# A graph attention layer on one core: the first turn waits for the one-hot, and SyncE fetches the rows of one tile in every 14th pair

## The chip, the cores and the metric

One core of one Trainium2 chip runs the kernel. The metric is the device time of one execution in microseconds (us); lower is better. The engines are TensorE (PE; its weight loads are listed apart as PEld), VectorE (DVE), ScalarE (ACT), GpSimd (POOL) and SyncE (SP). A DMA is issued by an engine's queue (SPq, ACTq, POOLq) and carried by the core's 16 DMA engines.

## The reference

12500 nodes with 128 features, 400000 edges sorted by their destination, 32 features an edge, 8 heads of 16 channels. Cut to what matters:

```python
x_l = (ln1(h) @ W_l).reshape(n, 8, 16)          # h = relu(layernorm(x))
x_r = (ln1(h) @ W_r).reshape(n, 8, 16)
e = (ea @ W_e).reshape(-1, 8, 16)               # each edge; each node has a loop with the mean of ea as well
m = leaky_relu(x_l[src] + x_r[dst] + e, 0.2)
alpha = einsum('ehc,hc->eh', m, att)
a = softmax of alpha over the edges of each dst
out = segment_sum(x_l[src] * a[:, :, None], dst, n) + bias
h = h + out
ff = gelu(ln2(h) @ W1 + b1) @ W2 + b2
return x + h + ff
```

## The kernel before

**Prologue.** For about 190 us the node statistics are made, the lists of sources and destinations come in, and x_l is written to a table in DRAM, `xl_dram`, one row of 512 bytes for each node.

**Edges.** The edges are cut into tiles of 128 and pairs of 512 (four tiles, j = 0 to 3); there are 782 pairs. Four pairs share one set of loads ("windows"), eight pairs make one batch of the softmax. A round is the time step of the schedule, one for each pair: `window_edges` writes the order of all engines out by hand, round by round, and each step has its own lag against the pair it works on. A tile framework turns the reads and writes into semaphore waits. Each engine carries out its own instructions strictly in order. What happens to pair c:

- *windows* (SP, round c-4, for four pairs at once): `words` reads the offset of the four pairs into a register (L1000, a TENSOR_LOAD), then come the DMAs of edge features `ea` (L1069), local destinations `dl` (L1074) and x_r's rows `zw` (L1079), each into one of a few buffers that TensorE has to have freed.
- *gather* (POOL, four rounds ahead or more): one indirect DMA for each tile (L1033) takes 128 rows of `xl_dram` into the slot of the pair in `ring`, which has 30 slots. A slot is free when the sums of the pair 30 before are done. 29 pairs, the "raw" ones, get their rows by one plain DMA of SP in place of the four gathers.
- *place* (DVE, round c-1): the one-hot of the destinations is written beside the edge features in `ea` (L1100).
- *combine* (PE, round c): four "turns" transpose the four tiles of gathered rows into a bank of PSUM (L1127), and one product of `zw` with `ea` closes z = x_l[src] + x_r[dst] + ea W_e in the same bank (L1132). The profile counts each z product as two instructions and each sum of a tile as two.
- *slope* (ACT, L1150), *bend* (DVE, L1164) and *score* (PE, L1185) are the leaky relu and the product with att.
- For each batch of eight pairs: scans over the sorted edges (DVE, L1193 to L1214), the exponential (ACT, L1218), the turn of the weights back (PE `t`, L1225) and a copy of them (ACT, L1235).
- *times* (DVE, L1246, round c+12): the rows in the ring are multiplied by their weights, in place, 512 columns in one operation.
- *collect* (PE, L1277, round c+13): the weighted rows are summed over destinations, into `sums`; ACT copies these to `rec` (L1289), and a DMA on ACT's queue (L1308), 24 rows at an address from a register, brings them to `state`.

Beside this run the steps of the groups of nodes (x_r for later nodes, and the feed-forward part for nodes that are done), with loads and stores of their own on SP's queue.

A "tell" is a semaphore increment by which an instruction says that it is done. The framework gives one to each instruction that another engine's instruction waits for.

Of the kernel before, what the change touches and what calls it, by code (L numbers as in the profile page):

```python
# [13 lines left out]
F32 = mybir.dt.float32  # L14
# [53 lines left out]
BUSY = 5  # L68
LEAD = 2
KEPT = 7  # L70
BIG = 2.0**100
CAP = 2.0**120

# [59 lines left out]
def raw_pairs(nt, n_edges):  # L133

    n_pr = -(-n_edges // (UP * U))
    at = [xr_round(t, nt, n_edges) + XR_STEPS + 1 + RAW_LATER for t in range(GN, nt, GN)]
    at = at[:-1] + [r + RAW_SHIFT for r in at[:RAW_MORE]]
    return [(r + RAW_STEPS + AHEAD + 1, r) for r in at if r + RAW_STEPS + AHEAD + 2 < n_pr]


def heads_of(nc, pool, out, att_c, fh):
# [8 lines left out]
def tile_gnn(  # L150
# [56 lines left out]
    idx_sb = keep.tile([P, IDX, NB * K], I32, name="idx_sb")  # L207
    NQU = NU // QU
    at_sb = keep.tile([1, NQU + BEHIND, 1 + QP], I32, name="at_sb")
    dst_sb = keep.tile([P, NCH * K], I32, name="dst_sb")  # L210
    local_sb = dst_sb.bitcast(F32)
    flag = keep.tile([1, 1], I32, name="flag")
# [69 lines left out]
    def from_pairs(a, b):  # L282

        ps = once_ps.tile([P, GN * P], F32, name="w_ps")
        nc.tensor.matmul(ps[:, 0 : b - a], pick, firsts[:, a:b], start=True, stop=True)
        nc.vector.tensor_tensor(
            local_sb[:, a * K : b * K].rearrange("p (c j) -> p c j", j=K),
            dst_sb[:, a * K : b * K].rearrange("p (c j) -> p c j", j=K),
            ps[:, 0 : b - a, None].to_broadcast([P, b - a, K]),
            op=OP.subtract,  # L290
        )

    first_sb = build.tile([1, NU // UP], I32, name="first_sb")
# [497 lines left out]
    with tc.manual_schedule():  # L791
        load_first()
        make_identity(nc, ident)
        load_weights()
        load_x(0, min(GN, NT))
        load_raw()
        load_x(GN, min(3 * GN, NT - GN))
        for t in range(4 * GN, NT, 14):
            load_x(t, min(14, NT - t))
        load_dst()  # L800
        load_consts()
        nc.vector.memset(empty, 0.0)
        rows_at = [i * 5 // 4 for i in range(len(raw))]
        for r in range(max(max(len(qs), 9) + LAST + 1, 16 + PARTS, rows_at[-1] + KEPT + 1)):
            if r == 0:
                count_up()
            for d, at in zip(raw, rows_at):
                if r == at:
                    raw_gather(d)
                if r == at + KEPT:  # L810
                    raw_store(d)
            if r == 3:
                weights()
            if r == 9:
                last_of_units()
            if r == 14:
                nc.sync.dma_start(src_sb, src)
                nc.sync.dma_start(
                    idx_sb[:, 0 : IDX - 1], src[:, 0 : (IDX - 1) * NB * K].rearrange("p (b k) -> p b k", b=IDX - 1)
                )  # L820
            if r == 10:
# [33 lines left out]
    with tc.If(fast == 1) as cmp:  # L855
        window_edges(
            tc, n_edges, ea_t, NT, NE, NUE, ident, wer, weh, zneg, nodes, local_sb, bias_r, b2_r, w1_sb, w2_sb,
            cols, xl_dram, xl_t, xr_dram, xr_t, dc_dram, g_dram, late_dram, state_dram, state, clear, xr_steps, qs, raw_steps, raw, x_t, out_t, bend_x, src, idx_sb, at_sb, wid,
        )
    with cmp.Else():  # L860
        with tc.tile_pool(name="any_h", bufs=1) as any_h:
# [69 lines left out]

def window_edges(
    tc, n_edges, ea_t, NT, NE, NUE, ident, wer, weh, zneg, nodes, local_sb, bias_r, b2_r, w1_sb, w2_sb,
    cols, xl_dram, xl_t, xr_dram, xr_t, dc_dram, g_dram, late_dram, state_dram, state, clear, xr_steps, qs, raw_steps, raw, x_t, out_t, bend_x, src, idx_sb, at_sb, wid,
):


# [41 lines left out]
    with ExitStack() as es:  # L979
# [25 lines left out]
        def rows_at(t, at, n, size):  # L1005

            return t.rearrange("n f -> (n f)").bitcast(U8)[ds(at, n * size)].rearrange("(n f) -> n f", f=size)

        def slot(c):
# [15 lines left out]
        def gather(c):  # L1025
            if c in of_raw:
                rows = nc.sync.dma_start(slot(c)[:, :, 0:P], late_dram[of_raw[c]["i"]])
                pairs[c]["rows"] = [rows.ins]
                return
            pairs[c]["rows"] = []  # L1030
            for t in tiles_of(c):
                for j in t:
                    rows = nc.gpsimd.indirect_dma_start(  # L1033
                        out=slot(c)[:, j, 0:P],
                        out_offset=None,
                        in_=xl_dram,
                        in_offset=bass.IndirectOffsetOnAxis(ap=index(c, j), axis=0),
                    )
                    behind_last(rows, c - RING)
                    pairs[c]["rows"].append(rows.ins)  # L1040
# [56 lines left out]
        def place(c):  # L1097

            d = pairs[c]
            placed = nc.vector.tensor_scalar(  # L1100
                d["ea"][0:WN].rearrange("p (a b) -> p a b", b=OW),
                d["dl"][0:WN].rearrange("p (a b) -> p a b", b=OS)[:, :, 0:OW],
                wid[0:WN], None, op0=OP.is_equal,
            )
# [17 lines left out]
        def combine(c):  # L1122
# [6 lines left out]
                ).ins  # L1129
                for j in range(e // P)  # L1130
            ]
            d["closed"] = nc.tensor.matmul(z[:, :e], d["zw"], d["ea"][:, :e], start=False, stop=True).ins  # L1132
            d["z"] = z
            for ins in d["loads"]:
# [105 lines left out]
        def times(c):  # L1240

            b, i = batch_at[c]
            weights = of_batch[b]["t"].rearrange("p (j w i h) -> p j w i h", j=KP, w=2, i=NB)[:, :, 0, i : i + 1]
            k = sum(len(t) for t in tiles_of(c))
            rows = slot(c)[:, 0:k, 0:P].rearrange("p j (c h) -> p j c h", h=H)
            product = nc.vector.tensor_tensor(  # L1246
                rows, rows, weights[:, 0:k].to_broadcast([P, k, C, H]), op=OP.mult
            )
            pairs[c]["products"] = [product.ins]
            for ins in (*pairs[c]["turns"], *pairs[c]["rows"]):  # L1250
                tc.declare_no_dep(
                    product.ins, ins, reason="TensorE waited for it ahead of the turned weights, which are read here"
                )

        def own_nodes(q):
            d = of_four[q]
# [932 lines left out]
```

## Time and profile before

| | |
|---|---|
| timed runs | 4845.96, 4851.8, 4852.41 us; median 4851.8 |
| the profiled execution | 4798.29 us, its span 4796.5 us |
| granted TensorE clock, mean | 0.875 |
| PE, DVE, POOL, ACT busy | 3544.8, 2622.4, 2952.7, 1502.6 us |
| DMA | 425616 packets, 536.78 MB, 112 GB/s |

How to read the lines below: a group of instructions is given as line, engine, operation, output <- input and count, then busy time and mean ns of one, then the idle time of the engine just before them and what ended most of it. In the chain that ended last each piece is followed back to what released it; "issue" is time in which an engine waited for nothing that the profile shows, "remote" or "another core or an unknown queue" a wait whose releaser the profile cannot name. A row of one line has the durations as min/median/max in ns. A row of windows has start and end, length, busy time with the number of instructions for each engine, granted clock, share of the DMA engines and GB/s. A row of the waits has total us, times and the longest.

### The profile page before, as it was taken

What the parts mean: (1) busy time and instruction counts of PE and PEld (TensorE: products, weight loads), DVE (VectorE), ACT (ScalarE), POOL (GpSimd) and SP (SyncE); (2) the same over time, 40 slices, a digit from 0 to 9 for tenths busy, and PEclk for the clock granted to TensorE, in tenths of its full rate; (3) what the DMA queues carried; (4) which work ended last, traced back from release to release, by engine and by line L of the source; (5) the groups of instructions that cost most, each with busy time, mean ns of one, the idle gap of its engine ahead of it and who ended that gap; (6) DMA issues with size and microseconds to landing.
All of it is one profiled execution on the core that took longest, in us unless ns stands there. A gap on an engine that the chain in (4) does not pass through costs nothing.

```text
span 4796.5 us, 48948 instructions
## 1 busy us (share of the span) xinstructions
PE 3544.8 (74%) x14951; PEld 1790.8 (37%) x14952; DVE 2622.4 (55%) x4977; ACT 1502.6 (31%) x3825; POOL 2952.7 (62%) x3136
## 2 busy tenths in 40 slices
PE   3327777777777777777777877777778777777787
PEld 2203333333333333343333433333434333333344
DVE  5316555655655555556555555555555555555455
ACT  5302323322322323323333333333333333333222
POOL 6655666665666666666666666666666666666650
PEclk8658888888888989899898989898989898889898
DMA  6525555555543443444434334343344433434331
GB/s 185 164 75 151 141 145 144 148 146 147 142 132 93 112 110 102 104 112 105 106 93 106 100 98 102 98 101 101 91 99 108 100 100 98 102 86 103 100 96 31
DMA packets 425616, 536.78 MB, mean 112 GB/s; under 512 B 97241, under 2 KB 307210, under 8 KB 424794
## 3 DMA queue, kind: packets, MB, share of 16 engines
q1 hardware_dynamic: 282360, 266.19, 21.5%
q0 software_dynamic: 100000, 205.00, 16.5%
q10 hardware_dynamic: 42984, 62.37, 4.4%
q8 instruction: 121, 1.98, 0.2%
q14 instruction: 151, 1.24, 0.1%
HBM read 471.82 MB, written 61.42 MB: 111 GB/s over the span
## 4 chain that ended last, share of the span: by engine, by line
PE 38%; DVE 20%; another core or an unknown queue 15%; issue 12%; ACT 5%; DMA 2%; POOL 1%; ACTq 1%; SPq 0%; DVEq 0%; POOLq 0%
PE sums L1277 12%; PE z L1132 9%; PE s L1185 7%; PE z L1127 6%; DVE ea L1100 3%; DVE ring L1246 3%; DVE m L1164 3%; DVE s L1193 2%; DVE p L1207 2%; POOL ring L1033 1%; DVE p L1200 1%; ACT zs L1150 1%; ACT rec L1289 1%; PE acc L1612 1%
## 5 line engine op out<-in xcount | busy, mean ns | idle before, releaser
L1033 POOL DMA_INDIRECT ring<-xl_dram,idx_sb x3009 | 2839.8, 944 | 1637.4 <-issue 785.4
L1277 PE MATMUL sums<-ring,own 128*32 128x144 f32 x6250 | 1044.9, 317 | 979.2 <-ACT rec L1289 645.2
L1277 PEld LDWEIGHTS sums<-ring,own 128*32 128x32 f32 x6250 | 681.8, 119 | 1551.7 <-ACT rec L1289 801.2
L1164 DVE TENSOR_TENSOR m<-z,zs 128x512 f32<-128x512 f32 x782 | 532.8, 681 | 900.7 <-issue 538.8
L1132 PE MATMUL z<-ea,zw 128*128 128x512 f32 x1564 | 920.2, 674 | 10.9 <-issue 7.4
L1185 PE MATMUL s<-m,zneg 128*64 128x512 f32 x1564 | 851.2, 636 | 90.9 <-issue 71.4
L1150 ACT ACTIVATE zs<-z 128x512 f32<-128x512 f32 x782 | 464.8, 594 | 1171.5 <-PE z L1132 303.7
L1246 DVE TENSOR_TENSOR ring<-ring,t 128x512 f32<-128x512 f32 x782 | 527.8, 676 | 391.8 <-PE t L1225 179.4
L1127 PE MATMUL z<-ident,ring 128*128 128x128 f32 x3125 | 594.1, 320 | 25.2 <-DMA raw_dram<-raw 11.5
L1100 DVE TENSOR_SCALAR ea<-dl,wid 96x516 f32<-96x516 bf16 x782 | 577.7, 739 | 15.1 <-DMA zw<-xr_dram 15.1
L1289 ACT COPY rec<-sums 32x144 f32<-32x144 f32 x782 | 204.8, 262 | 1103.7 <-remote 332.0
L1127 PEld LDWEIGHTS z<-ident,ring 128*128 128x128 f32 x3125 | 379.8, 158 | 243.0 <-issue 218.1
L1185 PEld LDWEIGHTS s<-m,zneg 128*64 128x64 f32 x1564 | 165.7, 142 | 758.2 <-issue 635.0
L1193 DVE TENSOR_TENSOR_SCAN s<-g,s 64x512 f32<-64x512 bf16 x98 | 120.4, 1228 | 332.0 <-remote 100.6
L1132 PEld LDWEIGHTS z<-ea,zw 128*128 128x128 f32 x1564 | 279.3, 223 | 11.9 <-issue 8.0
L1259 DVE TENSOR_TENSOR own<-nodes,sums 128x512 f32<-128x512 f32 x195 | 132.6, 680 | 246.3 <-remote 190.0
L1218 ACT ACTIVATE p<-p 64x512 f32<-64x512 f32 x98 | 61.7, 630 | 330.0 <-DVE p L1207 128.8
L1235 ACT COPY ring<-t 128x256 f32<-128x256 f32 (+3 forms) x236 | 65.7, 344 | 253.7 <-DVE ring L1246 150.6
L326 POOL DMA_INDIRECT raw<-in_x,lead x92 | 88.9, 967 | 52.0 <-issue 26.6
L1207 DVE TENSOR_TENSOR_SCAN p<-g,s 64x512 f32<-64x512 bf16 x98 | 119.8, 1222 | 1.5
L1336 DVE TENSOR_REDUCE part<-ea_s 128x1 f32<-128x1024 f32 x98 | 118.3, 1207 | 0.0
L1218 ACT ACT_TABLE_LOAD x66 | 84.7, 1283 | 1.2
(244 smaller groups left out, 2248.5 us busy)
## 6 DMA issues: line engine op xcount, KB each, us to landing
dl<-dc_dram SPq DMA_DIRECT2D x196, 396.0 KB
ea_s<-in_ea_t ACTq DMA_DIRECT2D x98, 512.0 KB
ea<-in_ea_t SPq DMA_DIRECT2D x196, 256.0 KB
ring<-xl_dram,idx_sb POOLq DMA_INDIRECT x3009
state<-empty SPq DMA_DIRECT2D x98, 144.0 KB
f_st<-state SPq DMA_DIRECT2D x48, 288.0 KB
state<-rec ACTq DMA_DIRECT2D x782, 13.5 KB
zw<-xr_dram SPq DMA_DIRECT2D x196, 48.0 KB
```

What stands on the lines that cost most here:

```text
L1033: rows = nc.gpsimd.indirect_dma_start(out=slot(c)[:, j, 0:P], out_offset=None, in_=xl_dram, in_offset=bass.IndirectOffsetOnAxis(ap=index(c ...
L1100: placed = nc.vector.tensor_scalar(d["ea"][0:WN].rearrange("p (a b) -> p a b", b=OW), d["dl"][0:WN].rearrange("p (a b) -> p a b", b=OS)[:, ...
L1127: nc.tensor.matmul(z[:, j * P : (j + 1) * P], row_of(c, j)[:, 0:P], ident, start=(j == 0), stop=False, is_transpose=True).ins
L1132: d["closed"] = nc.tensor.matmul(z[:, :e], d["zw"], d["ea"][:, :e], start=False, stop=True).ins
L1150: sloped = nc.scalar.activation(d["zs"][:, :e], d["z"][:, :e], AF.Copy, scale=SLOPE)
L1164: bent = nc.vector.tensor_tensor(d["m"][:, :e], d["z"][:, :e], d["zs"][:, :e], op=OP.max)
L1185: d["score"] = nc.tensor.matmul(of_batch[b]["s"][0:HB, :e], zneg[:, k : k + HB], d["m"][:, :e], start=(i == 0), stop=(c == batches[b][-1]) ...
L1193: nc.vector.tensor_tensor_scan(d["s"][HB:P], d["g"][:, 0:EPR], d["s"][0:HB], BIG, op0=OP.add, op1=OP.min)
L1207: nc.vector.tensor_tensor_scan(d["p"][0:HB, back], d["g"][:, 1 : EPR + 1][:, back], d["s"][HB:P][:, back], BIG, op0=OP.add, op1=OP.min)
L1246: product = nc.vector.tensor_tensor(rows, rows, weights[:, 0:k].to_broadcast([P, k, C, H]), op=OP.mult)
L1277: nc.tensor.matmul(sum_at[c % PLACES], own[:, c % QP * KP + j, :], slot(c)[:, j, :], start=(j == js[0]), stop=(j == js[-1]),).ins
L1289: nc.scalar.copy(d["rec"], sum_at[c % PLACES])
```

## The change

**The first turn waits.** `place` keeps its instruction, and `combine` gives the first turn of each pair a dependency on it. The product that closes z then has nothing left to wait for. With that most turns lose their tells: in the two built programs the turns tell 2286 times before and 159 times after, and TensorE in all 5254 and 3148 times.

On PE, around one pair of z bank 1653 to 1655 (before), with the semaphores that each row waits for (DMASW: a gather has landed; DVE, Activation: VectorE, ScalarE):

```order
1790 L1277 MATMUL sums<-ring,own 32x144 x3
1791 L1127 MATMUL z_1655<-ident,ring 128x128 [waits DMASW4_49]
1792 L1127 MATMUL z_1655<-ident,ring 128x128 [waits DMASW5_49]
1793 L1127 MATMUL z_1655<-ident,ring 128x128 [waits DMASW6_49]
1794 L1127 MATMUL z_1655<-ident,ring 128x128 [waits DMASW7_49]
1795 L1132 MATMUL z_1655<-ea,zw_1645 128x512 [waits DVE_49]
1796 L1277 MATMUL sums<-ring,own 32x144 [waits DVE_49,Activation_49]
```

The same place after, where turns are L1210, the closing product L1220 and the sums L1373:

```order
1796 L1373 MATMUL sums<-ring,own 32x144 x3
1797 L1210 MATMUL z_1662<-ident,ring 128x128 [waits DMASW7_49,DVE_49]
1798 L1210 MATMUL z_1662<-ident,ring 128x128 [waits DMASW0_49]
1799 L1210 MATMUL z_1662<-ident,ring 128x128 [waits DMASW1_49]
1800 L1210 MATMUL z_1662<-ident,ring 128x128 [waits DMASW2_49]
1801 L1220 MATMUL z_1662<-ea,zw_1652 128x512
1802 L1373 MATMUL sums<-ring,own 32x144 [waits DVE_49,Activation_49]
```

VectorE's wait has moved from the closing product to the first turn; a second semaphore of one instruction takes an extra step in the queue, and there are 605 of these before the turns after the change (26 before).

**Rows by hand.** For the pairs 30, 44, 58, ... (54 of them) the fourth tile is not gathered by GpSimd. SyncE fetches its 128 rows with 128 DMAs of one row (512 bytes), each at an address from a register, into one of three tiles `hand0` to `hand2`. The addresses come from `hand_sb`, a list of offsets that is built in the prologue (a memset and a copy on DVE, a transpose on PE, a product on DVE), 16 at a time by a TENSOR_LOAD. The rows of a tile are spread over 14 rounds, from 20 to 7 rounds ahead of its pair, half of a round's nine or so at its start and half at its end. One round ahead of the pair SP waits until all 128 have landed. The fourth turn reads the hand tile, and `times` becomes two operations, one of three tiles and one of the hand tile into the ring. In all 6912 row DMAs, 432 loads of 16 words, and 54 gathers less.

On SP, from one windows step to the next (L1000 is `words`, L767 clears state, L685 loads x_r rows), before:

```order
242 L1000 TENSOR_LOAD at_sb
243 L1069 DMA ea<-in_ea_t 32x4x512 [waits DMAHW5_49,PE_49]
244 L1074 DMA dl_1647<-dc_dram 96x2112 [waits DMAHW0_49]
245 L1079 DMA zw_1646<-xr_dram 96x512 [waits DMAHW1_49]
246 L767 DMA state<-empty 128x2x144 [waits DMAHW2_49]
247 L685 DMA xr_4398<-raw_dram 128x512 [waits DMAHW6_49,PE_49,Activation_49]
248 L1000 TENSOR_LOAD at_sb
249 L1069 DMA ea<-in_ea_t 32x4x512 [waits DMAHW1_49,PE_49]
```

and such a stretch after (L1044 is `words`, L1082 a row by hand, L1152 to L1162 the windows, L805 and L723 as L767 and L685):

```order
384 L1152 DMA ea<-in_ea_t 32x4x512 [waits DMAHW7_49,DVE_49,PE_49]
385 L1157 DMA dl_1654<-dc_dram 96x2112 [waits DMAHW0_49]
386 L1162 DMA zw_1653<-xr_dram 96x512 [waits DMAHW1_49]
387 L1082 DMA hand_6198<-xl_dram 1x512 x5
388 L805 DMA state<-empty 128x2x144 [waits DMAHW2_49]
389 L1082 DMA hand_6198<-xl_dram 1x512 x7
390 L1044 TENSOR_LOAD hand_sb
391 L1082 DMA hand_6198<-xl_dram 1x512 x16
392 L1044 TENSOR_LOAD hand_sb
393 L1082 DMA hand_6198<-xl_dram 1x512 x8
394 L723 DMA xr_6513<-raw_dram 128x512 [waits DMAHW1_49,PE_49,Activation_49]
395 L1044 TENSOR_LOAD at_sb
```

36 rows and two loads of offsets now stand between the windows of four pairs and the next.

The diff, cut to its core:

```diff
+HAND_LEAD = 6
+HAND_READ = 16
+HAND_EVERY = 14
+HAND_FIRST = 30
+LANDED = 7
...
+        def hand(r, w, share=(0, 1), behind=0):
+            hands, n = w["pairs"], w["sems"]
+            i, k = divmod(r + HAND_LEAD + hands.step - hands[0], hands.step)
+            if share[0] == 0:
+                w["new"].clear()
+                if k == HAND_LEAD - 1 and 0 < i <= len(hands):
+                    all_here = w["queue"].wait_ge(w["landed"][(i - 1) % n], ((i - 1) // n + 1) * P * 16)
+                    tc.declare_fence(all_here.ins, group=f"{w['name']}{i - 1}")
...
+            first, last = P * k // hands.step, P * (k + 1) // hands.step
+            for e in range(*(first + int((last - first) * x) for x in share)):
+                if e % HAND_READ == 0:
+                    d["at"] = words(
+                        hand_sb[w["at"] + i : w["at"] + i + 1, e : min(e + HAND_READ, P)], (NT * P - 1) * XW * 4,
+                        w["engine"],
+                    )
+                row = w["queue"].dma_start(
+                    d["x"][e : e + 1, :].bitcast(U8), rows_at(xl_dram, d["at"][e % HAND_READ], 1, XW * 4)
+                )
+                row.then_inc(w["landed"][i % n], 16)
...
         def row_of(c, j):
-            return slot(c)[:, j, 0:P]
+            return by_hand[c]["x"] if c in by_hand and j == KP - 1 else slot(c)[:, j, 0:P]
...
                 for j in t:
+                    if c in by_hand and j == KP - 1:
+                        continue
                     rows = nc.gpsimd.indirect_dma_start(
...
-            placed = nc.vector.tensor_scalar(
+            d["placed"] = placed = nc.vector.tensor_scalar(
...
+            tc.add_manual_dep(
+                nc.get_inst_by_name(d["turns"][0].name), d["placed"].ins.name,
+                mybir.DependencyInfo(mybir.DependencyClass.Sync, mybir.DependencyReason.DATA),
+                reason="the product that closes z reads the one-hot and waits for nothing itself",
+            )
             d["closed"] = nc.tensor.matmul(z[:, :e], d["zw"], d["ea"][:, :e], start=False, stop=True).ins
...
+            n = sum(len(t) for t in tiles_of(c))
+            whole = n - 1 if c in by_hand else n
+            for js, x in ((slice(0, whole), None), (slice(whole, n), by_hand.get(c))):
...
+                product = nc.vector.tensor_tensor(
+                    rows,
+                    rows if x is None else x["x"][:, None, :].rearrange("p j (c h) -> p j c h", h=H),
+                    weights[:, js].to_broadcast([P, k, C, H]),
+                    op=OP.mult,
+                )
...
             for r in range(-AHEAD, max(last_round, groups[-1]["round"] + 19)):
+                hand(r, ways[0], (0, 0.5))
                 in_round(r, early, groups[:-2])
...
+                hand(r, ways[0], (0.5, 1))
```

More of the change, by code (lines that the diff above doesn't have):

```diff
@@ L70 @@
 KEPT = 7
+HAND_LEAD = 6
[3 more added lines that the diff above has]
+LANDED = 7
+HAND_ROUND = 24
 BIG = 2.0**100
@@ L138, in raw_pairs, with hand_pairs @@
     return [(r + RAW_STEPS + AHEAD + 1, r) for r in at if r + RAW_STEPS + AHEAD + 2 < n_pr]
+def hand_pairs(nt, n_edges):
+    late = {c for c, _ in raw_pairs(nt, n_edges)}
+    hands = range(HAND_FIRST, n_edges // (UP * U), HAND_EVERY)
+    assert not late & set(hands)
+    return hands
 def heads_of(nc, pool, out, att_c, fh):
@@ L290, in from_pairs, with hand_columns, hand_turn, hand_bytes @@
             op=OP.subtract,
+        )
+    hand_f = build.tile([P, len(hands)], F32, name="hand_f")
+    hand_ps = {}
+    def hand_columns():
+        nc.vector.memset(hand_f, 0.0)
+        for at, h in ((0, hands),):
+            first = (h[0] + 1) * UP * KU - 1
+            step = h.step * UP * KU
+            nc.vector.tensor_copy(
+                hand_f[:, at : at + len(h)], src_sb[:, first : first + step * (len(h) - 1) + 1 : step]
+            )
+    def hand_turn():
+        hand_ps["t"] = once_ps.tile([P, GN * P], F32, name="w_ps")
+        nc.tensor.transpose(hand_ps["t"][0 : len(hands), 0:P], hand_f, ident)
+    def hand_bytes():
+        nc.vector.tensor_scalar(
+            hand_sb, hand_ps["t"][0 : len(hands), 0:P], float(XW * 4), None, op0=OP.mult
         )
@@ L857, in tile_gnn @@
             tc, n_edges, ea_t, NT, NE, NUE, ident, wer, weh, zneg, nodes, local_sb, bias_r, b2_r, w1_sb, w2_sb,
-            cols, xl_dram, xl_t, xr_dram, xr_t, dc_dram, g_dram, late_dram, state_dram, state, clear, xr_steps, qs, raw_steps, raw, x_t, out_t, bend_x, src, idx_sb, at_sb, wid,
+            cols, xl_dram, xl_t, xr_dram, xr_t, dc_dram, g_dram, late_dram, state_dram, state, clear, xr_steps, qs, raw_steps, raw, x_t, out_t, bend_x, src, idx_sb, at_sb, hand_sb, hands, wid,
         )
@@ L933, in window_edges @@
     tc, n_edges, ea_t, NT, NE, NUE, ident, wer, weh, zneg, nodes, local_sb, bias_r, b2_r, w1_sb, w2_sb,
-    cols, xl_dram, xl_t, xr_dram, xr_t, dc_dram, g_dram, late_dram, state_dram, state, clear, xr_steps, qs, raw_steps, raw, x_t, out_t, bend_x, src, idx_sb, at_sb, wid,
+    cols, xl_dram, xl_t, xr_dram, xr_t, dc_dram, g_dram, late_dram, state_dram, state, clear, xr_steps, qs, raw_steps, raw, x_t, out_t, bend_x, src, idx_sb, at_sb, hand_sb, hands, wid,
 ):
@@ L1007, in rows_at @@
             return t.rearrange("n f -> (n f)").bitcast(U8)[ds(at, n * size)].rearrange("(n f) -> n f", f=size)
+        ways = (
+            {"pairs": hands, "at": 0, "queue": nc.sync, "engine": SP, "name": "hand", "sems": LANDED, "new": []},
+        )
+        by_hand = {c: {} for w in ways for c in w["pairs"]}
+        for w in ways:
+            w["landed"] = [tc.alloc_semaphore(f"{w['name']}_landed{i}") for i in range(w["sems"])]
+        def hand(r, w, share=(0, 1), behind=0):
[6 more added lines that the diff above has]
+                    tc.declare_fence(all_here.ins, group=f"{w['name']}{i - 1}")
+            i, k = divmod(i * hands.step + k - behind, hands.step)
+            if not 0 <= i < len(hands):
+                return
+            d = by_hand[hands[i]]
+            if k == 0 and share[0] == 0:
+                d["x"] = once.tile([P, XW], F32, name=f"{w['name']}{i % 3}")
+            first, last = P * k // hands.step, P * (k + 1) // hands.step
[7 more added lines that the diff above has]
+                    d["x"][e : e + 1, :].bitcast(U8), rows_at(xl_dram, d["at"][e % HAND_READ], 1, XW * 4)
+                )
+                row.then_inc(w["landed"][i % n], 16)
+                tc.no_tile_sem_insts.add(row.ins.name)
+                tc.add_to_no_dep_group(f"{w['name']}{i}", row.ins)
+                w["new"].append(row)
         def slot(c):
@@ L1243, in times @@
             weights = of_batch[b]["t"].rearrange("p (j w i h) -> p j w i h", j=KP, w=2, i=NB)[:, :, 0, i : i + 1]
[L1244 to L1252, printed above, removed]
-                )
+            n = sum(len(t) for t in tiles_of(c))
+            whole = n - 1 if c in by_hand else n
+            for js, x in ((slice(0, whole), None), (slice(whole, n), by_hand.get(c))):
+                k = js.stop - js.start
+                if k == 0:
+                    continue
+                rows = slot(c)[:, js, 0:P].rearrange("p j (c h) -> p j c h", h=H)
+                product = nc.vector.tensor_tensor(
[3 more added lines that the diff above has]
+                    op=OP.mult,
+                )
+                pairs[c].setdefault("products", []).append(product.ins)
+                for ins in (*pairs[c]["turns"], *pairs[c]["rows"]):
+                    tc.declare_no_dep(
+                        product.ins, ins, reason="TensorE waited for it ahead of the turned weights, which are read here"
+                    )
         def own_nodes(q):
```

10 lines of the change are left out of this document (added).

## The prediction

> **What bounds the kernel now.** I read the page first: busy time, the chain that ended last, the costly groups.
>
> ```profile
> span 4796.5 us, 48948 instructions
> PE 3544.8 (74%) x14951; PEld 1790.8 (37%) x14952; DVE 2622.4 (55%) x4977; ACT 1502.6 (31%) x3825; POOL 2952.7 (62%) x3136
> ...
> PE 38%; DVE 20%; another core or an unknown queue 15%; issue 12%; ACT 5%; DMA 2%; POOL 1%; ACTq 1%; SPq 0%; DVEq 0%; POOLq 0%
> ...
> L1033 POOL DMA_INDIRECT ring<-xl_dram,idx_sb x3009 | 2839.8, 944 | 1637.4 <-issue 785.4
> L1277 PE MATMUL sums<-ring,own 128*32 128x144 f32 x6250 | 1044.9, 317 | 979.2 <-ACT rec L1289 645.2
> ...
> L1132 PE MATMUL z<-ea,zw 128*128 128x512 f32 x1564 | 920.2, 674 | 10.9 <-issue 7.4
> ...
> L1150 ACT ACTIVATE zs<-z 128x512 f32<-128x512 f32 x782 | 464.8, 594 | 1171.5 <-PE z L1132 303.7
> L1246 DVE TENSOR_TENSOR ring<-ring,t 128x512 f32<-128x512 f32 x782 | 527.8, 676 | 391.8 <-PE t L1225 179.4
> L1127 PE MATMUL z<-ident,ring 128*128 128x128 f32 x3125 | 594.1, 320 | 25.2 <-DMA raw_dram<-raw 11.5
> L1100 DVE TENSOR_SCALAR ea<-dl,wid 96x516 f32<-96x516 bf16 x782 | 577.7, 739 | 15.1 <-DMA zw<-xr_dram 15.1
> ...
> L1127 PEld LDWEIGHTS z<-ident,ring 128*128 128x128 f32 x3125 | 379.8, 158 | 243.0 <-issue 218.1
> ```
>
> No engine is full. The chain is 38% TensorE, 20% VectorE, and 27% time in which the trace names no worker ("another core or an unknown queue", "issue"). TensorE idles 979.2 us ahead of the sums, mostly for ScalarE's rec, and ScalarE idles 1171.5 us ahead of the slope, mostly for TensorE's z. So the pace is a loop of short steps handed between engines, and how soon a handover arrives matters.
>
> One such handover, from the timeline:
>
> ```profile
> 2523.13 1.02 PE L1132 MATMUL z<-ea,zw 128*128 128x512 f32 x2
> ...
> 2526.02 0.27 ACT L1289 COPY rec<-sums 32x144 f32<-32x144 f32 x1 [4.58 <-PE s L1185]
> ...
> 2531.66 0.60 ACT L1150 ACTIVATE zs<-z 128x512 f32<-128x512 f32 x1 [5.38 <-remote]
> ...
> 2533.06 1.23 DVE L1193 TENSOR_TENSOR_SCAN s<-g,s 64x512 f32<-64x512 bf16 x1 [10.88 <-remote]
> ```
>
> The product z is over at 2524.15, the slope that reads it begins at 2531.66 though ScalarE had nothing to do for 5.38 us. The records end early or TensorE's tell arrives late; nothing else is named.
>
> Then the pace, by windows over one stage (first the closing products alone, then the gathers alone):
>
> ```profile
> 1500.00:2500.00 1000.00, 203.89 (x350) 61.26 (x348) 0.90 0.41 106
> 1500.00:2500.00 1000.00, 640.83 (x681) 0.90 0.41 106
> ```
>
> 350 halves of z are 175 pairs in 1000 us: 5.71 us a pair, 80 us for 14 pairs. A gather costs GpSimd 0.944 + 785.4/2554 = 1.25 us, so 681 take 851 us: GpSimd has 15% to spare. What it waits for says the same:
>
> ```profile
>   PE sums L1277: 190.6, 47
> ...
>   PEld z L1127: 13.0, 29
> ```
>
> It stands still because a ring slot is not yet free (first line), while the turns wait only 13.0 us in all for gathered rows (second line). The gathers run ahead; they do not set the end.
>
> **The first turn waits for the one-hot, and turns tell no more.** Who waited for the one-hot:
>
> ```profile
>   PEld z L1132: 3.9, 1
>   PE z L1132: 3.5, 1
> ```
>
> One wait of 3.9 us in 782 products: VectorE places a pair a round ahead, so moving this wait four turns (about 1 us) earlier costs nothing and its removal from z gains at most 4 us; I put 0. Behind the waiting turn stand z, the score and the next sums, so if VectorE fell behind by more than it does now, all of them would wait; the cover is VectorE's 45% of idle time.
>
> What changes is how many times TensorE tells: counted in the two built programs, the semaphore increments fall from 5254 to 3148, those of the turns from 2286 to 159: 2127 fewer. No row prices one tell. From below: nothing, since a group of four turns, each telling, is not issued wider than untold ones (only 25.2 us of idle before 3125 turns). From above: a semaphore step on TensorE's own queue,
>
> ```profile
> L1277 PEldq EVENT_SEMAPHORE  x489: 51/51/51, 368.5 to 4754.9; - x163
> ```
>
> 51 ns, 2127 × 0.051 = 108 us. A tell sits on the same engine, so I price it at this row, and count it where TensorE is on the chain: 38% of 108 = **-41 us**. A loss by fewer tells I exclude: nobody waits for a turn alone but the ring's next gather and VectorE's product, both of which wait for later work anyway. The page "TensorE: Matmul & The Clock Gate", section "The cost: per-tile semaphore tail", of the Trainium skill gives about 26 ns for each increment of a tile's tail and calls a single one on the last matmul sound; by it the term would be 38% of 56, -21 us, and no row here tells the two prices apart.
>
> The price for it: the first turn now waits for two semaphores (gather and one-hot), and the second costs a step of its own in the queue: 605 more, × 51 ns = 31 us. Hidden where the queue runs ahead of the array; the weight load of the turns idles 218.1 us by "issue" in some 750 gaps, so it is not always ahead. Between 0 and 31, again by the chain's 38%: **+12 us**.
>
> **54 tiles fetched by SyncE.** GpSimd drops 54 of 3009 gathers, 54 × 1.25 = 67 us of its time. It waits for ring slots, so this becomes more waiting: **0** (bounds 0 and -67).
>
> VectorE multiplies such a pair in two operations, three tiles and one. A 512-column product takes 676 ns; two of 384 and 128 share the columns, and the second adds a fixed part that no row isolates; between 0 and a quarter of the whole (169 ns). 54 × 0.169 = 9 us at most, by VectorE's 20% of the chain **+2 us**. The four operations that build the list of offsets stand in the prologue, once, beside the node statistics' 128-row work: 0. The bytes: 54 × 64 KB in 6912 packets against 425616 packets now: 0.
>
> SyncE is the open question. It gets 6912 one-row DMAs and 432 loads of 16 words; each tile's are spread over 14 pairs' time. Rows for its prices:
>
> ```profile
> L1000 SPq TENSOR_LOAD <-at_sb x196: 3/412/1009, 194.6 to 4692.9; - x196
> L1000 ACTq TENSOR_LOAD <-at_sb x196: 485/1100/1399, 374.8 to 4760.8; - x196
> ...
> L1308 ACTq DMA_DIRECT2D state<-rec x782: 307/309/1126, 377.7 to 4764.7; - x196
> ...
> L1069 SPq DMA_DIRECT2D ea<-in_ea_t x196: 157/334/656, 195.4 to 4701.8; - x196
> L1074 SPq DMA_DIRECT2D dl<-dc_dram x196: 310/423/962, 195.7 to 4702.2; - x196
> L1079 SPq DMA_DIRECT2D zw<-xr_dram x196: 3/352/1449, 196.8 to 4702.7; - x196
> ...
> SPq L1069 <- PE z L1132: 746.1, 63, 22.3
> ```
>
> A row's DMA: nearest is the state write at a register's address, 24 rows, 309 ns (ends 157 and 423). A load: one word 0.41 us, four words (on ScalarE) 1.10, at best 0.485; so 0.12 to 0.28 us a word, 1.9 to 4.4 us for 16. SyncE's own work: per four pairs 0.41 + 0.33 + 0.42 + 0.35 = 1.5 us, 5.3 per 14, and its other moves about as much again; I put 12 us. In 80 us then: 128 × 0.309 = 40, eight loads 16 to 35, own 12: 68 to 87 us. At the ends of the DMA's price 48 to 101. The nearest row with the smaller load fits, with the larger it doesn't. I take that it fits, since SyncE today waits at the windows until TensorE frees a buffer (last row, up to 22.3 us at a time): its loads come a whole four of pairs early, and a lateness below that is free: **0**. What is queued behind the rows on SyncE: the windows of four pairs (with about 37 rows and two or three loads between them), limits, indices, the clearing of state, the group's loads and stores. The wait for a landed tile comes five rounds (28 us) after its last row was issued: 0.
>
> **Sum.** -41 + 12 + 2 = -27 us: the profiled execution of 4798.29 us (span 4796.5 and 1.8 around it) would become 4771. That execution is 1.1% under the median of the timed runs, 4851.8; the same step from there gives **4825 us**.
>
> **Rivals.**
> 1. *SyncE becomes the bound* (slower). Place: its queue between two windows. It decides once rows, loads and own work pass 80 us per 14 pairs, that is, with rows at 309 ns, loads above 3.5 us. At 4.4 us the excess is 7 us for each of 54 tiles: +378, 5230 us. If only now and then a window comes late, 1 to 2 us for each tile: 4906 to 4960. For it: the median of four words; SyncE works in order, so rows stand still whenever a window waits. Against: waits of up to 22.3 us ahead of the windows now. The page "Runtime: NRT & Kernel Launch" of the Trainium skill, section "Instruction fetch mechanics", gives about 200 ns for each register loaded, even in bulk; by that a load is 3.2 us, the sum 78 of 80 us, which speaks against the change more than the small end of my rows does.
> 2. *The tells cost nothing* (no change): issue does not widen for them, and the 27% without a named worker has another cause. +12 at most, +2 at least: 4854 to 4866; or 4852 with the queue's steps hidden too.
> 3. *GpSimd counts after all* (faster). If ring waits fed back into the gathers' start, 67 us less: 4851.8 - 67 - 27 = 4758 us. Against: 13.0 us of turns waiting for rows.
> 4. *The second semaphore in full*, 31 us, with no gain: 4885 us.
>
> **How the numbers follow.** Forecast 0.44, with a range of its own from 4790 to 4850; rival 1 0.22, half of it above 4960; rival 2 0.18; rival 3 0.10; rival 4 0.06. About 10 us (0.2%) is what a measurement of this kernel can tell from no change. Faster: 0.40 of the forecast and rival 3, 0.50; same: 0.04 and 0.16 of rival 2, 0.20; slower: the rest, 0.30. The range goes down to the tells at their full 108 us (4851.8 - 108 + 2 = 4746) and up to the milder form of rival 1 (4960); some 0.16 lies outside.
>
> **What would show it.** Right: the closing product has no idle time by VectorE, ScalarE's waits for z and rec shrink by some tens of us, the gathers' idle time ahead of ring slots grows by about 67 us, SyncE's longest waits for z at the windows shrink but stay. Wrong: the one-hot or z waits for the DMAs of ea, dl or zw (rival 1), turns wait for SyncE's landed tile, the turns' weight loads idle more by "issue" (rival 4), or the span falls with the gathers (rival 3). The prediction fails most likely on the price of a 16-word load or of a tell, neither of which this trace holds.

## The result, and the profile after

The changed kernel took 5476.7 us (median of 4, 5462.14 to 5484.27) where the kernel before took 4848.88 on the same chip: ratio 1.130, 95% interval 1.127 to 1.133. It is 13% slower. I had forecast 4825 us, a little faster, with a range up to 4960: wrong in sign and by far in size.

One thing has to be known for all that follows. The experiments ran on chips of two kinds. On one kind the kernel before takes 4781 to 4849 us, on the other 3989 to 3990, with the same program. I call them the slower and the faster chip. They are different chips: of those with a number on record, 1, 7 and 11 were of the faster kind, 0, 9 and 15 of the slower. The forecast, its trace and the result above are of the slower kind; the number of that chip is not on record. Each ratio is against the kernel before, measured beside it on the same chip.

The page of the changed kernel, lines that answer to those before:

```profile
span 5475.5 us, 63991 instructions
PE 3693.7 (67%) x14952; PEld 1854.0 (34%) x14953; DVE 2629.5 (48%) x5034; ACT 1488.8 (27%) x3825; POOL 2900.8 (53%) x3082
...
L1116 POOL DMA_INDIRECT ring<-xl_dram,idx_sb x2955 | 2787.3, 943 | 2359.8 <-PE sums L1373 1095.0
...
L1238 ACT ACTIVATE zs<-z 128x512 f32<-128x512 f32 x782 | 464.0, 593 | 1844.2 <-DMA state<-empty 670.2
L1220 PE MATMUL z<-ea,zw 128*128 128x512 f32 x1564 | 962.0, 702 | 2.1 <-issue 2.0
...
L1183 DVE TENSOR_SCALAR ea<-dl,wid 96x516 f32<-96x516 bf16 x782 | 578.4, 740 | 489.1 <-DMA zw<-xr_dram 281.1
...
L1210 PE MATMUL z<-ident,hand 128*128 128x128 f32 x54 | 21.0, 389 | 162.8 <-SPq L1067 92.5
...
PE 2%; SPq 1%; DVE 1%; issue 1%; ACT 0%; DMA 0%; POOL 0%; ACTq 0%; DVEq 0%
```

The last line is the chain that ended last. Here it breaks off after 5% of the span, so it doesn't name what sets the pace; the waits have to. TensorE's busy time grew by 149 us, at a granted clock of 0.835 in place of 0.875, and that of the other engines hardly moved; the rest of the loss is waiting. The gathers wait longer for the ring (1637.4 us of idle became 2359.8), so GpSimd is further from the end than before. The one-hot, which idled 15.1 us, now idles 489.1, mostly for `zw` to arrive: a windows load comes late. The hand tile itself is late too: its turns idle 162.8 us, mostly for SyncE's wait (L1067). The one-hot's wait for `zw` and the turns' wait for the hand tile were the signs I had named for SyncE as the bound. The closing product idles 2.1 us, as planned.

SyncE's queue, waits and instructions of the changed kernel:

```profile
SPq L1152 <- remote: 114.6, 5, 72.9
...
SPq L1152 <- PE z L1220: 12.2, 6, 8.0
...
L1044 SPq TENSOR_LOAD <-hand_sb x432: 3/1247/1561, 358.7 to 5341.2; - x144
...
L1082 SPq MOVE hand<-xl_dram x6912: 1/29/1452, 360.0 to 5350.1; - x198
L1082 SPq DMA_DIRECT2D hand<-xl_dram x6912: 1/228/1466, 360.1 to 5350.2; - x198
```

At the windows SyncE used to wait 746.1 us for z; 12.2 are left. The 114.6 us stand almost wholly before the first row. All waits of SyncE's queue together fall from 2908 to 356 us. It has hardly any slack left, and the rows run from 360 to 5350 us with no gap above 11 us. A row is two instructions, a MOVE of 29 ns and a DMA of 228, by their medians; but the maxima are 1.45 us for either. The medians mislead: in this stretch of the timeline (start, length, line, count)

```profile
2507.75 9.07 SPq L1082 DMA_DIRECT2D hand<-xl_dram  x12
```

twelve rows take 9.07 us, 0.76 us a row. From the start of one row to the start of what follows it, over all 6912 rows, the mean is 0.531 us; for the loads of 16 words it is 1.14. So a tile costs SyncE 128 × 0.531 + 8 × 1.14 = 77 us. Its other work takes 11.8 us more, and on semaphores it waits 3.6, together 92.4 us ((5350 - 360)/54), for 14 pairs that took 80 us before. A queue that waits 3.6 of 92.4 us is full: that is the new pace.

### The profile page after: what moved, and what is told of

It reads as the page before. It is cut to its first block, busy times and chain, and to the rows that moved or that the text cites. A ratio compares the mean times of both kernels' runs of the same rounds, so it can differ in the third digit from the quotient of the medians.

```text
span 5475.5 us, 63991 instructions
## 1 busy us (share of the span) xinstructions
PE 3693.7 (67%) x14952; PEld 1854.0 (34%) x14953; DVE 2629.5 (48%) x5034; ACT 1488.8 (27%) x3825; POOL 2900.8 (53%) x3082
## 5 line engine op out<-in xcount | busy, mean ns | idle before, releaser
L1116 POOL DMA_INDIRECT ring<-xl_dram,idx_sb x2955 | 2787.3, 943 | 2359.8 <-PE sums L1373 1095.0
L1373 PE MATMUL sums<-ring,own 128*32 128x144 f32 x6250 | 1078.9, 324 | 1215.9 <-ACT rec L1385 718.4
L1373 PEld LDWEIGHTS sums<-ring,own 128*32 128x32 f32 x6250 | 699.0, 122 | 1833.6 <-ACT rec L1385 967.9
L1220 PE MATMUL z<-ea,zw 128*128 128x512 f32 x1564 | 962.0, 702 | 2.1 <-issue 2.0
L1273 PE MATMUL s<-m,zneg 128*64 128x512 f32 x1564 | 878.8, 656 | 98.8 <-issue 81.2
L1183 DVE TENSOR_SCALAR ea<-dl,wid 96x516 f32<-96x516 bf16 x782 | 578.4, 740 | 489.1 <-DMA zw<-xr_dram 281.1
L1210 PE MATMUL z<-ident,ring 128*128 128x128 f32 x3071 | 604.7, 328 | 111.1 <-DVE ea L1183 75.2
L1339 DVE TENSOR_TENSOR ring<-ring,t 128x512 f32<-128x512 f32 (+1 forms) x782 | 520.9, 667 | 286.8 <-PE z L1220 79.2
L1210 PEld LDWEIGHTS z<-ident,ring 128*128 128x128 f32 x3071 | 384.7, 162 | 335.7 <-issue 232.6
L1220 PEld LDWEIGHTS z<-ea,zw 128*128 128x128 f32 x1564 | 294.7, 234 | 1.8 <-issue 1.8
L1281 DVE TENSOR_TENSOR_SCAN s<-g,s 64x512 f32<-64x512 bf16 x98 | 120.0, 1225 | 163.9 <-remote 71.0
L1210 PE MATMUL z<-ident,hand 128*128 128x128 f32 x54 | 21.0, 389 | 162.8 <-SPq L1067 92.5
```

What stands on the lines that cost most here:

```text
L1116: rows = nc.gpsimd.indirect_dma_start(out=slot(c)[:, j, 0:P], out_offset=None, in_=xl_dram, in_offset=bass.IndirectOffsetOnAxis(ap=index(c ...
L1183: d["placed"] = placed = nc.vector.tensor_scalar(d["ea"][0:WN].rearrange("p (a b) -> p a b", b=OW), d["dl"][0:WN].rearrange("p (a b) -> p ...
L1210: nc.tensor.matmul(z[:, j * P : (j + 1) * P], row_of(c, j)[:, 0:P], ident, start=(j == 0), stop=False, is_transpose=True).ins
L1273: d["score"] = nc.tensor.matmul(of_batch[b]["s"][0:HB, :e], zneg[:, k : k + HB], d["m"][:, :e], start=(i == 0), stop=(c == batches[b][-1]) ...
L1281: nc.vector.tensor_tensor_scan(d["s"][HB:P], d["g"][:, 0:EPR], d["s"][0:HB], BIG, op0=OP.add, op1=OP.min)
L1339: product = nc.vector.tensor_tensor(rows, rows if x is None else x["x"][:, None, :].rearrange("p j (c h) -> p j c h", h=H), weights[:, js] ...
```

## The experiments

Theory S: SyncE's queue is full and sets the pace. Rival T: the first turn's wait makes the loss. Rival D: the rows' DMAs slow all other work in proportion to their number.

**The first turn alone.** The list of hand pairs is empty, and its prologue steps are gone:

```diff
-    hands = range(HAND_FIRST, n_edges // (UP * U), HAND_EVERY)
+    hands = range(HAND_FIRST, HAND_FIRST, HAND_EVERY)
```

> The first turn's wait alone, no rows by SyncE: all gathers stay with GpSimd. Theory S (SyncE's queue is full and sets the pace: 128 rows at 0.53 us, eight loads at 1.14 us and 16 us of own work are 93 us for 14 pairs that took 80): the loss is gone, 4800 to 4870 us. Rival T (the loss is the first turn's: a wait in front of it holds up the queue of TensorE, with 605 double waits): 5400 us or more. Rival D (each row's DMA, with its packet and its semaphore writes, slows all other work in proportion to their number): 4800 to 4870. Within S and D the run also prices the fewer tells: 4811 if my term of -41 us holds with 0 for the queue's steps, 4850 if tells cost nothing, 4880 if the double waits cost their 31 us.

> The first turn alone once more. Faster chip: 3989 us, as before. Slower chip: S 4780 to 4870; T (the turn's wait makes the loss): 5400 or more.

The first run fell on the faster chip: 3988.51 us, ratio 0.9998 (0.9989 to 1.0007). The second fell on the slower one: 4842.91, ratio 0.9996 (0.9978 to 1.0013). T falls, and with it my gain: in both runs the turns tell 2127 times less, and the turns' extra steps for a second semaphore grow by 579 (605 after less 26 before), and together this changes nothing on either chip, to 0.2%. On the faster chip the page of this run names GpSimd, by its chain and by the turns, which wait for gathered rows:

```profile
PE 35%; POOL 20%; DMA 17%; issue 12%; DVE 9%; ACT 2%; ACTq 1%; SPq 0%; POOLq 0%; DVEq 0%
...
L1203 PE MATMUL z<-ident,ring 128*128 128x128 f32 x3125 | 591.3, 302 | 243.6 <-DMA ring<-xl_dram,idx_sb 237.7
```

**The rows alone**, without the dependency in `combine`:

```diff
-            tc.add_manual_dep(
-                nc.get_inst_by_name(d["turns"][0].name), d["placed"].ins.name,
...
```

> The rows by SyncE alone, the first turn without its dependency, so the closing product waits for the one-hot again. S and D: as the changed kernel, 5430 to 5530 us. T: near the kernel before, 4830 to 4900.

4029.09 us on the faster chip, 1.0106 (1.0090 to 1.0121). My numbers were for the other chip; the next run gives the one to compare with.

**The changed kernel again.**

> The changed kernel itself, beside the kernel before on the chip of this call. The chip of the first experiments ran the kernel before in 3989 us where the first one took 4849, and a row of SyncE took 0.34 us there against 0.53. If this call's chip is like the slower one: 5477 us, ratio 1.13. If it is like the faster one: SyncE needs 128 x 0.34 + 8 x 1.33 + 16 = 70 us for 14 pairs, and the kernel before takes some 66: about 4030 us, ratio 1.01, like the rows alone did there.

4032.7 us on the faster chip, 1.0106 (1.0089 to 1.0123). The rows alone give the same, so the whole loss is the rows' there. On the slower chip the rows alone were not run; that the loss is theirs there too follows from the first turn alone, which costs nothing, unless the two act only together. And the same program loses 1% on one chip and 13% on the other. Its SyncE rows on the faster chip:

```profile
L1044 SPq TENSOR_LOAD <-hand_sb x432: 1157/1268/1723, 207.8 to 3898.2; - x144
L1082 SPq MOVE hand<-xl_dram x6912: 29/29/39, 209.2 to 3906.5; - x198
L1082 SPq DMA_DIRECT2D hand<-xl_dram x6912: 221/228/555, 209.2 to 3906.6; - x198
...
PE 28%; SPq 25%; DVE 13%; DMA 11%; issue 10%; POOL 5%; ACT 4%; ACTq 1%; POOLq 0%; DVEq 0%
```

The medians are those of the slower chip (29 and 228 ns), but no MOVE is above 39 ns and no row's DMA above 555. A row takes 0.340 us from start to start, a tile with SyncE's other work 68.5 us ((3906.6 - 209.2)/54); SyncE's queue holds 25% of the chain.

**Fewer loads of offsets**: the first 16 offsets are used for all 128 rows.

```diff
-                if e % HAND_READ == 0:
+                if e == 0:
```

> The rows' offsets are loaded once for a tile in place of eight times, and the 16 offsets are used again for all 128 rows (wrong rows, the same DMAs). S: 7 x 1.14 = 8 us less for each tile, 85 of 80 us, so 54 x 8 = 430 us less: 5000 to 5100 us. D and T: the DMAs and the turns are the same, 5430 to 5530.

3926.73 us on the faster chip, 0.9842 (0.9827 to 0.9857): it gains. The expected times were for the slower chip, where it was not run. Each tile is rid of 7 × 1.34 = 9 us on SyncE, 68.5 becomes 59 by this count, where 14 pairs now take 66, and the row queue fits. Then the 54 gathers show: 54 × 1.25 = 67 us were to be had, 62.6 are measured.

**Fewer tiles.** In every 28th and in every 18th pair:

```diff
-HAND_EVERY = 14
+HAND_EVERY = 28
```

> A tile in every 28th pair: 27 tiles, 3456 rows, each tile's rows spread over 28 rounds. S: SyncE has 68 + 9 us of rows and loads and 32 us of own work in 28 pairs' 160 us, 109 in all, so it no longer sets the pace and nearly all of the loss is gone: 4820 to 4920 us. D: half of the rows, half of the loss, about 5160. T: 5477 as before.

> A tile in every 28th pair. Slower chip: SyncE has 128 x 0.61 + 8 + 32 = 118 us in 28 pairs' 160 us: no longer full, but trains of rows still make a window late now and then: 4850 to 4920 us. Rival D (each row costs the others): half of 628, 5160. Faster chip: 3957 us again.

> A tile in every 28th pair. Slower chip: 128 x 0.61 + 8 + 32 = 118 us of SyncE's work in 28 pairs' 160 us, so SyncE is no longer full, but a window comes late now and then: 4820 to 4900 us where the kernel before takes 4790 to 4850, a ratio of 1.00 to 1.02. If each row cost the others in proportion: 1.065. Faster chip: 3957 us again.

> A tile in every 18th pair (42 tiles), correct rows. Faster chip (before 3990): SyncE has 43 + 11 + 21 = 75 us of work in 18 pairs' 85 us, so the row queue fits, and GpSimd, which sets the pace there, is rid of 42 gathers at 1.25 us: 3990 - 52 = 3938 us. If it were not GpSimd's time that counts: 3990. Slower chip (before 4850): 68 + 9 + 21 = 98 of 103 us, near the edge: 4850 to 5000.

> A tile in every 18th pair. Slower chip: 5030 us again. Faster chip: 43 + 11 + 21 = 75 us of SyncE's work in 85 us, 42 gathers at 1.25 us gained: 3938 us.

| tile in every | tiles | faster chip | slower chip |
|---|---|---|---|
| no pair (first turn alone) | 0 | 3988.51, 0.9998 | 4842.91, 0.9996 |
| 28th | 27 | 3956.58, 0.9919 (0.9904 to 0.9934); 3958.23, 0.9923 | 4862.12, 1.0169 (1.0151 to 1.0187) |
| 18th | 42 | 3938.21, 0.9869 (0.9853 to 0.9886) | 5031.52, 1.0403 (1.0388 to 1.0417) |
| 14th | 54 | 4032.7, 1.0106 | 5476.7, 1.130 |

On the faster chip the gain is 33, 31 and 51 us for 27, 27 and 42 tiles, 1.1 to 1.2 us a gather, until SyncE is full; then it is lost at once. Every 18th pair beats both kernels there by 1.3% to 2.3%, as worked out before it ran (3938). On the slower chip it loses 4%, so no version that ran on both is better on both; 5031 us is also above the 4850 to 5000 that were expected. The loss there is not proportional to the rows (81, 192, 628 us for 3456, 5376, 6912), which is what a queue that fills does and D doesn't. SyncE's time for one tile on the slower chip, worked out from the records, in us:

| tile in every | rows | loads | other work | waits on semaphores | sum |
|---|---|---|---|---|---|
| 28th | 86.5 | 8.4 | 32.5 | 36.5 | 163.9 |
| 18th | 79.0 | 8.3 | 16.0 | 6.6 | 109.9 |
| 14th | 67.9 | 9.1 | 11.8 | 3.6 | 92.4 |

In the 18th the queue is as good as full, in the 28th it is not. So the foot of the loss is not explained by S: with 27 tiles no window is late after the first 309 us (until then the one-hot idles 51.6 us, where it was 15.1, and that is made up: the 100th pair or so is closed at 857 us, before at 859), and 81 us are lost all the same. What costs them stays open.

**Two rows in one DMA.**

```diff
+                if e % 2:
+                    continue
...
-                    d["x"][e : e + 1, :].bitcast(U8), rows_at(xl_dram, d["at"][e % HAND_READ], 1, XW * 4)
+                    d["x"][e : e + 2, :].bitcast(U8), rows_at(xl_dram, d["at"][e % HAND_READ], 2, XW * 4)
```

> Every 14th pair again, but each DMA brings two neighbouring rows, so 64 DMAs for a tile with the same eight loads and the same bytes (every second row is another than wanted). S: SyncE saves 64 x 0.34 = 22 us for a tile on the faster chip, 48 of 66 us: the queue fits, and 54 gathers at 1.25 us are gained, 3922 us. On the slower chip it saves 34 of 92 us: near the kernel before, 4830 to 4880. D (packets and bytes): the same loss as the changed kernel, 4033 or 5477.

4892.82 us on the slower chip, 1.0115 (1.0097 to 1.0133), where 5477 was the changed kernel's. The same bytes for half of the DMAs, and nine tenths of the loss are gone, where a cost in proportion to the DMAs would leave half: it is SyncE's time that costs. A DMA took 0.71 us in the mean, a tile's 64 of them 45 us in place of 68, and SyncE's queue waited 10.5 of 81.5 us for each tile. It ended 13 us above what S expected; like the 81 us in the table above, this remainder is not explained.

**What makes a row long on the slower chip.** I sorted the 5957 rows that another row follows at once by how many gathers GpSimd had begun between 4 and 1 us earlier. Mean time of a row from start to start in ns, and number of rows, worked out from the records of the changed kernel on both chips:

```
gathers begun     slower chip          faster chip
0                 339 (1275 rows)      334 (18 rows)
1                 346 (1634)           338 (66)
2                 641 (2421)           337 (3569)
3                 959 (627)            339 (2304)
```

On the slower chip a row behind two or three gathers is two to three times as long; on the faster chip, where the gathers come more densely, nothing. That gave theory G: on the slower chip a train of GpSimd's gathers holds up the other engines' queues. Against it stands that SyncE may be slow there whatever GpSimd does. The test leaves out the gathers of every second pair, in the kernel before and after:

```diff
+                    if c >= 60 and c % 2 == 0:
+                        continue
                     rows = nc.gpsimd.indirect_dma_start(
```

> The kernel before, with the gathers of every second pair left out from pair 60 on (those pairs work on old rows; nothing else is left out). Theory G (on the slower chip GpSimd's gathers hold up the other engines' queues, SyncE's instructions and TensorE's tells): there, fewer standstills, 4300 to 4650 us; rival (GpSimd is off the path there and does not disturb): 4800 to 4850. On the faster chip, where the trace of the first turn alone has GpSimd on the chain: TensorE's loop sets the pace, 3700 to 3900 us.

> The kernel before with the same gathers left out. Slower chip: G, if the same trains also hold back TensorE's tells: 4300 to 4650 us; rival: 4800 to 4850. Faster chip: 3762 us again.

> The kernel before with the same gathers left out. Slower chip: G, if the same trains also hold back TensorE's tells: 4300 to 4650 us; rival: 4800 to 4850. Faster chip: 3762 to 3770 us.

> The changed kernel with the same gathers left out. Slower chip: G: half of the rows at 0.34 us in place of 0.7 or more, SyncE's 92 us for 14 pairs become 80 or fewer: 4750 to 5050 us; rival: 5430 to 5520. Faster chip: SyncE has the same work, and sets the pace: 4000 to 4050 us though GpSimd is idle half of the time.

> The changed kernel with the gathers of every second pair left out. Slower chip: theory G (gathers in a train make the long instructions on SyncE): fewer than half of the long rows, a row at some 0.45 us, 58 + 9 + 16 = 83 us for 14 pairs against 92: 4750 to 5050 us; rival (that chip's SyncE is slow whatever GpSimd does): 5430 to 5520. Faster chip: 4019 us again.

> The changed kernel with the gathers of every second pair left out. Slower chip: theory G (trains of gathers make the long instructions): 4750 to 5050 us, the rows' mean near 0.45 us; rival (that chip's SyncE is slow whatever GpSimd does): 5430 to 5520, mean 0.53. Faster chip: 4013 to 4019 us.

| gathers of every second pair left out | faster chip | slower chip |
|---|---|---|
| in the kernel before | 3762.36, 0.9426; 3770.0, 0.9456 | 3922.87, 0.819 (0.817 to 0.821) |
| in the changed kernel | 4019.25, 1.0074; 4012.75, 1.0064 | 4411.06, 0.921 (0.915 to 0.927) |

On the faster chip the changed kernel stays at 4013 to 4019 us though GpSimd has half of its gathers: SyncE alone sets the pace there. On the slower chip both kernels get far faster, by more than I expected (both are below their ranges): the kernel before by 864 us. SyncE's rows fell from 0.531 to 0.386 us, so most of what they had above 0.34 us was the gathers'. The changed kernel's SyncE stays full, at 73 us a tile with 2 of waiting. The pace was not GpSimd's (its gathers waited for ring slots) and half of its gathers were nevertheless worth 18%. The chain of the kernel before with half of the gathers, on the slower chip:

```profile
PE 59%; DVE 20%; issue 6%; ACT 4%; another core or an unknown queue 4%; ACTq 1%; DMA 1%; SPq 0%; DVEq 0%; POOLq 0%; POOL 0%
```

"Another core or an unknown queue" and "issue", 27% of the chain before (1295 us), are 10% here (392 us), and 16% (628 us) in the run with plain DMAs that follows: at least half of the standstills without a named worker went with half of the gathers.

**The rows' bytes or the gathers.** In every second pair one plain DMA of SyncE brings 512 rows in place of four gathers:

```diff
+            if c >= 60 and c % 2 == 0:
+                rows = nc.sync.dma_start(
+                    slot(c)[:, :, 0:P], xl_dram[c % 16 * UP * U : (c % 16 + 1) * UP * U].rearrange("(j p) f -> p j f", p=P)
+                )
...
```

> The kernel before; in every second pair from 60 on the four gathers are replaced by one plain DMA of SyncE that brings 512 rows of 512 bytes from a fixed place of the same table (other rows than wanted, the same bytes). Slower chip: if the rows' traffic disturbs, 4700 to 4850 us, as with all gathers; if the gathers of GpSimd themselves do, 3920 to 4050. Faster chip: 3770 to 3850 us, as with the gathers left out, and a little more for SyncE's DMAs.

3929.2 us on the slower chip, 0.820 (0.818 to 0.823), the same as with no rows at all. So the bytes into the ring cost nothing here, and the gathers, as GpSimd issues them, are what disturbs. The plain DMA reads 512 neighbouring rows where a gather reads scattered ones; whether that matters, what else in a gather does it, and why one chip shows it and the other not, was not tested. The granted clock goes with it (0.867 on the slower chip and 0.941 on the faster for the first turn alone, 0.933 on the slower one with half of the gathers), but by TensorE's busy time it is not the main part: for the first turn alone TensorE is busy 191 us longer on the slower chip, whose span is 861 us longer.

## Why the prediction was wrong

- **The step that failed: SyncE's term, put at 0.** I had 40 + 16 to 35 + 12 = 68 to 87 us for 14 pairs and took that it fits into 80. It measured 68 + 9 + 12 = 89, and with 3.6 us of waiting 92.4. The loads were below my lower end (1.14 us in place of 1.9 to 4.4), the own work was right (12); the failing number is the row, 0.309 taken from ScalarE's write, 0.531 measured. My upper end for a row, 0.423, was too low as well; the 92 lies inside my widest sum, 48 to 101, only because the loads were put too high there. I had named the load and the tell as the likeliest to fail, not the row. On the faster chip the row (0.340) and the sum (68.5) come out at the low end of mine; but the pace is faster there too, so it overflows by little.
- **Why the row was mis-sized.** I took a median from a line whose own maximum stood beside it (307/309/1126). Of SyncE's and ScalarE's lines in the trace before, several had such tails (the load of one word 3/412/1009, the zw DMA 3/352/1449). A full queue pays the mean, tails included, and each row also has a MOVE, which I left out. But that is only part of it: by the records of the trace before, the mean of ScalarE's write was 0.372 us, with its MOVE 0.401, still well below 0.531. The rest is what the gathers do to SyncE's rows on this chip; no row of the trace before shows it, and the test with half of the gathers does.
- **The slack.** SyncE's waits for z (746.1 us) I read as room. They were, and 12.2 us were left of them; but a queue is judged by its sum against the pace, and mine straddled it: "I take that it fits" chose one side without a row that decides. The bounds and the tipping point of rival 1 were right (loads and rows above 80 us decide); its chance of 0.22 and its upper time of 5230 were too low, since I let only the loads vary.
- **Tells and double waits**, -41 and +12 us: the sum of -29 us is refuted by both runs of the first turn alone, which measure nothing to 0.2%; whether each is nothing or the two cancel, the runs don't show. The double waits were also miscounted: 605 is their number after, 579 is the growth, so 30 us in place of 31. Rival 2, that the tells cost nothing, fits best. By the Trainium skill's price for an increment ("TensorE: Matmul & The Clock Gate", "The cost: per-tile semaphore tail") the term was -21 us, with the +12 -9 us: the run on the slower chip can't tell that from nothing (its interval reaches to -11 us), the one on the faster chip, which reaches to -4 us, doesn't show it.
- **The gathers**, 0: right on the slower chip for the reason given, GpSimd waits for ring slots. On the faster chip they set the pace and 1.1 to 1.2 us each came back, so rival 3 is true there. What I missed on the slower one is that an engine off the chain disturbs the others: half of its gathers cost 18%. The 27% of the chain without a named worker was the place to ask.
- **The 16-word load**: 1.25 us by the median, 78 ns a word. The Trainium skill ("Runtime: NRT & Kernel Launch", "Instruction fetch mechanics") gives about 200 ns for each register loaded, which would be 3.2 us. The trace of these loads, whose words lie in the tile `hand_sb` and not in DRAM, does not agree, and the measurement decides. The rule spoke for the right outcome by the wrong term.

## What to carry to other kernels

Before work is moved to an engine that "only issues DMAs", sum its queue over one period, with all instructions of a step and with mean times and not medians, and compare with the pace; even so the sum is a lower bound if another engine can hold up the queue, as here; if the sum's range holds the pace, a small step past it can cost far more than the move can gain (here 628 us against 67). If much of the chain has no named worker, find out what runs when everything stands still: a run that left out half of one engine's work told what no waiting line did. Price an offload by the chip at hand: here the same program lost 1% on one kind and 13% on the other.

## What the runs showed of the hardware

- In the changed kernel a one-row DMA at a register's address occupied SyncE for 0.34 us with its MOVE, on either chip, with no gather begun 4 to 1 us before; behind two or three gathers it took 0.64 to 0.96 us on the slower chip and still 0.34 on the faster.
- On the slower chip half of the gathers less was worth 864 of 4787 us, and with as many rows by plain DMAs in their place 862 of 4791 us.
- A TENSOR_LOAD of 16 words took 1.25 to 1.27 us on SyncE by the median, one word 0.41 (before) to 0.47 (after).
- 2127 semaphore increments of TensorE fewer, with 579 more steps for a second semaphore, changed the time by no more than 0.2%.
